# A two-layer transformer block on one core: another hand-written order for the drain of the attention and for the routed feed-forward behind it

## The chip, the core and the metric

The kernel runs on one core of a Trainium2 chip. TensorE (PE) multiplies matrices and transposes by multiplying with an identity; its results land in PSUM, a small memory which the kernel here cuts into buffers of 512 fp32 per partition. VectorE (DVE), ScalarE (ACT) and GpSimd (POOL) work on 128 partitions at a time; SyncE (SP) issues most of the transfers. Each engine runs its own list of instructions strictly in the order in which the kernel wrote them, and waits at an instruction until what it needs is there. The metric is device time in microseconds (us) from the first to the last instruction with what lies around it, here the median of several runs.

## The reference, cut to what matters

The input is `x`, 2 batches of 512 rows of 512 numbers. Two layers follow one another, each an attention and a feed-forward, each of these behind a layer norm that is scaled and shifted by numbers made from a conditioning vector (`mod`) and added to `x` through a gate. The change touches the last part of layer 1 only: the end of its attention, and its feed-forward.

```
h = layernorm(x) * (1 + cb) + sb
base_out = h @ base_W.T + base_b
probs = softmax(h @ router_W.T + router_b)        # 15 routes per row
topk_p, topk_i = top_k(probs, 8)
w = topk_p spread to the 8 experts by expert_map[topk_i]
lora = ((h @ A[e].T) * w[e]) @ B[e].T * 2          # rank 16 per expert, 8 experts
x = x + gb * (base_out + lora)
```

The attention of layer 1 has 128 heads with 4 numbers each, a latent of 64 and a rotary part of 64, and no mask; its scores are `exp(s - max)` and the sum is divided out at the end.

## The kernel before, in words

**Attention of layer 1.** The heads are taken four at a time in 64 units, called quads `t`; `Z` is the last one, `Z - 1` the one before it. A quad has four key blocks `i` and two pairs of heads `p`. For each `rope` multiplies the scores into PSUM (tile `s_i_p`, two halves of 512, pool `pS`, one buffer for each `p`), `keep` (ACT) copies them to SBUF, `largest` (DVE) takes the running maximum `mx`. When all blocks are in, `blocks`, `tops`, `twice` (DVE), `join` (a PE transpose), `top`, `top_hi`, `top_lo` (DVE) and `stripes` (POOL) bring the maxima into a layout from which `row` (PE) spreads each to a row `psm`; `row_copy` (ACT) makes SBUF copies of two of them. `less_...` subtracts the rows from the kept scores on DVE and POOL, `exponential` (ACT) follows, and `mix` (PE) multiplies with the values into `acc`. A planned order, `PLAN1`, lays the steps of neighbouring quads beside each other; `beside` hangs single steps of the feed-forward behind named steps of the plan near its end.

**The tail.** When the plan has run out, `tail()` lists by hand what is left, in the order in which every engine gets it: the end of quad `Z - 1`, the drain of quad `Z` (`part(i, odd)` does the subtractions and the exponentials of block `i`; with `odd`, DVE takes one more of the subtractions), `leave(Z)` and `last[...]`, which divide by the sums (`inverse`, `back`, `exact`, `spreading`, `scale`, `both`), then `projected(i)`, which multiplies with `Wo`, gates and adds to `x` for the four row tiles of batch 1.

**The feed-forward, class `Ffn1`.** Batch 0 has left the attention before, so its feed-forward can begin inside the drain; batch 1 has to wait for `projected`. For a batch `b`: `stats` (DVE) takes mean and variance of each row tile, `scale` (L370, L371) the root of the variance on ACT and its reciprocal on DVE, `rows(t)` (L385, DVE) the normalised rows `xn`; `turn(b, kc)` (L394 to L406) transposes them four tiles at a time on PE into a PSUM buffer and scales and shifts on the way out into `hT`, on ACT for even and on DVE for odd `kc`; `logits` (L412, 16 multiplications that the trace shows as 32 records) and `probs` (L433 to L437) make the exponentials of the routing; `chosen` (L444 to L464, DVE) normalises, compares each probability with each other (L451, 900 per partition) and counts ranks; `hidden` (L469) multiplies with the experts' first matrices; `weighed` (L485 to L490) turns the chosen weights and multiplies them in; `base(t)` (L499, 8 records) and `low(t)` (L509, 2 records) multiply into one PSUM tile per row tile, `leave(t)` (L520, L521) gates, adds and sends it out. `ready(f)` (L376) runs one tiny activation so that ACT loads the table of function `f` early.

**Buffers.** The pool `pX` has three PSUM buffers of 512 for everything small; `pS` has the two pairs of 512 that held the scores and later hold `base` and `low`. In the drain the rows `psm` 0 and 2 occupy two of the three `pX` buffers to the end, so the four transpositions of batch 0 share the third one.

**Where things stand before the change.** `scale(0)` hangs behind `exponential 0 0` of the plan, and `rows(0)`, `rows(1)` behind `tops 0`; `rows(2)`, `rows(3)` stand in the tail, ahead of `row`. The logits of batch 0 stand in one piece between `mix(Z, 1)` and `mix(Z, 2)`. `chosen(0)` stands in one piece between `scaled()` and `projected(0)`.

## Time and profile before

| what | value |
|---|---|
| runs | 2519.63, 2522.49, 2522.56 us; median 2522.49 us |
| the profiled execution | 2519.66 us, of which 2517.9 us are its span |
| mean granted TensorE clock | 0.985 |
| from 1000 to 2300 us | PE busy 1299.99 of 1300 us, clock 1.00 |
| from 2399 to 2439 us | PE busy 29.12 of 40 us, DVE 21.22, ACT 23.23, POOL 17.25, clock 0.68 |
| from 2439 to 2477 us | PE busy 31.06 of 38 us, DVE 25.43, ACT 6.39, POOL 11.15, clock 0.89 |
| from 2477 to 2518 us | PE busy 33.12 of 41 us, DVE 15.25, ACT 1.43, POOL 13.66, clock 0.85 |

The profile is one execution, recorded by the hardware. A page of it gives the busy time of each engine, and the chain that ended last, followed back from the last instruction: each piece of it is a start, a length and what ran then. A timeline lists the instructions of a stretch in order of time, with the wait ahead of each in brackets. A third view cuts a stretch into windows and gives for each the busy time of every engine and the granted TensorE clock as a share of full speed. Until 2399 us the core is bound by PE alone; the last 119 us are where the engines wait for each other, and the change lies in them.

### The profile page before, as it was taken

To read this page: it belongs to the slowest core of one execution; us is meant where nothing else is said; L and a number is where in the kernel's file an instruction comes from. 1 tells how busy PE (TensorE), PEld (TensorE's weight loads), DVE (VectorE), ACT (ScalarE), POOL (GpSimd) and SP (SyncE) were. 2 spreads that over 40 slices of the span, in tenths; PEclk is the share of its full clock that TensorE was granted. 3 is DMA by queue.
4 is the path that set the end of the run, shared out by engine and by line. 5 is a ranking of instruction groups with operands and counts; after the bars stand their busy time and mean duration, and the time that the engine had idled before them with its cause. 6 is when DMAs were issued, how large, how long until landed. Compare 5 with 4: busy or idle time off the path is not lost.

```text
span 2517.9 us, 28439 instructions
## 1 busy us (share of the span) xinstructions
PE 2453.7 (97%) x10252; PEld 1146.2 (46%) x10252; DVE 1684.2 (67%) x2309; ACT 1401.9 (56%) x2086; POOL 1571.9 (62%) x1521
## 2 busy tenths in 40 slices
PE   8999999999999899999999999999999999999877
PEld 3555555555555444444443444444344444444333
DVE  4445555555555435787778777778778877788764
ACT  2212112121221215888888788888888878888650
POOL 1333333333334323888888888888888888888643
PEclk9999999999999999999999999999999999999978
DMA  6211101001000100000000000000100000110000
GB/s 240 88 49 60 42 5 38 26 20 40 17 1 7 29 15 26 26 26 26 26 26 17 29 27 26 26 18 26 30 26 26 18 25 26 30 29 21 17 9 34
DMA packets 68697, 81.32 MB, mean 32 GB/s; under 512 B 6989, under 2 KB 49772, under 8 KB 68428
## 3 DMA queue, kind: packets, MB, share of 16 engines
q1 hardware_dynamic: 68348, 79.35, 10.1%
q8 instruction: 81, 1.33, 0.2%
q14 instruction: 60, 0.49, 0.1%
q0 software_dynamic: 208, 0.16, 0.0%
HBM read 77.40 MB, written 2.10 MB: 32 GB/s over the span
## 4 chain that ended last, share of the span: by engine, by line
PE 95%; DVE 3%; ACT 1%; DMA 0%; issue 0%; POOL 0%; SPq 0%; DVEq 0%; ACTq 0%; POOLq 0%
PE s L1081 19%; PE psq L1014 18%; PE acc L1236 10%; PE ps_q L685 9%; PE pw L797 8%; PE s L1090 5%; PE s L736 4%; PE po L783 4%; PE psv L707 2%; PE ps_k L685 2%; PE pt L772 2%; PE psu L1033 2%; PE psm L1160 2%; PE psw L1292 1%; PE psf L499 1%; PE psf L264 1%
## 5 line engine op out<-in xcount | busy, mean ns | idle before, releaser
L1187 POOL TENSOR_TENSOR ss<-ss,row 128x512 f32<-128x512 f32 x504 | 634.5, 1287 | 42.8 <-ACT row L1172 42.8
L1100 ACT COPY ss<-s 128x1024 f32<-128x1024 f32 x512 | 505.4, 1015 | 179.2 <-PE s L1090 130.5
L1081 PE MATMUL s<-q,ckr 64*128 64x512 f32 x2048 | 554.5, 612 | 10.7 <-ACT ss L1100 10.7
L1190 ACT ACTIVATE ss<-ss 128x1024 f32<-128x1024 f32 x512 | 525.2, 1070 | 5.6 <-DVE ss L1402 4.5
L1014 PE MATMUL psq<-hT,wqr 128*128 128x512 f32 x1024 | 466.7, 598 | 0.0
L1090 PE MATMUL s<-qm,c 64*128 64x512 f32 x1024 | 419.7, 795 | 0.4 <-DVE c L1051 0.4
L753 ACT ACTIVATE p<-s,nm 128x256 f32<-128x256 f32 (+1 forms) x256 | 110.9, 445 | 489.6 <-DVE nm L749 480.8
L1107 DVE TENSOR_TENSOR mx<-s,mx 128x1024 f32<-128x1024 f32 x256 | 306.6, 1218 | 41.2 <-PE s L1090 40.1
L695 POOL TENSOR_TENSOR qT<-t_q,t_q 128x512 f32<-128x512 f32 x64 | 81.2, 1269 | 402.6 <-DVE t_q L694 402.6
L1181 POOL TENSOR_TENSOR ss<-ss,rowe 128x512 f32<-128x512 f32 x252 | 317.9, 1285 | 0.0
L1014 PEld LDWEIGHTS psq<-hT,wqr 128*128 128x128 f32 x1024 | 189.0, 189 | 242.3 <-issue 211.7
L1081 PEld LDWEIGHTS s<-q,ckr 64*128 64x128 f32 x2048 | 184.1, 186 | 215.8 <-ACT ss L1100 97.3
L1236 PE MATMUL acc<-ss,vp 128*32 128x512 f32 x2048 | 266.9, 614 | 0.0
L1107 DVE TENSOR_TENSOR mx<-s,ss 128x1024 f32<-128x1024 f32 x128 | 156.7, 1224 | 117.1 <-ACT row L1172 79.7
L797 PE MATMUL pw<-wo,oT 128*128 128x512 f32 x512 | 230.3, 592 | 0.0
L685 PE MATMUL ps_q<-hT,wq 128*128 128x512 f32 x512 | 230.1, 592 | 0.0
L1112 DVE STREAM_TRANSPOSE mx<-mx 128x1024 f32<-128x1024 f32 x128 | 158.6, 1239 | 2.3
L1118 DVE TENSOR_REDUCE m<-mx 128x32 f32<-128x1024 f32 x128 | 156.1, 1219 | 4.4
L1090 PEld LDWEIGHTS s<-qm,c 64*128 64x128 f32 x1024 | 104.6, 187 | 118.8 <-issue 114.6
L1150 POOL TENSOR_TENSOR st<-mh,own_block 128x512 fp32r<-128x512 f32 x64 | 67.0, 1047 | 142.9 <-DVE mh L1146 142.9
L1183 DVE TENSOR_TENSOR ss<-ss,psm 128x512 f32<-128x512 f32 x252 | 155.7, 679 | 0.0
L685 PEld LDWEIGHTS ps_q<-hT,wq 128*128 128x128 f32 x512 | 96.0, 190 | 102.3 <-issue 100.6
(208 smaller groups left out, 3089.5 us busy)
## 6 DMA issues: line engine op xcount, KB each, us to landing
wqr<-in_L_attn_Wq_rope_pairs SPq DMA_DIRECT2D x64, 512.0 KB
wmod<-in_L_wmod SPq DMA_DIRECT2D x12, 1024.0 KB
wq<-in_L_attn_wq SPq DMA_DIRECT2D x8, 1024.0 KB
wo<-in_L_attn_wo SPq DMA_DIRECT2D x8, 1024.0 KB
x<-in_L_attn_x SPq DMA_DIRECT2D x8, 256.0 KB
wk<-in_L_attn_wk SPq DMA_DIRECT2D x8, 256.0 KB
wv<-in_L_attn_wv SPq DMA_DIRECT2D x8, 256.0 KB
out<-yf SPq DMA_DIRECT2D x8, 256.0 KB
```

The lines of the kernel that those rows point to most:

```text
L685: nc.tensor.matmul(ps, lhsT=wcols(kc), rhs=hT[b][:, kc, :], start=(kc == 0), stop=(kc == KC - 1))
L797: nc.tensor.matmul(ps, lhsT=oTs[u][:, hh, i * P : (i + 1) * P], rhs=groups[g]["o"][:, hh, :], start=(hh == 0), stop=(hh == GRP - 1),)
L1014: nc.tensor.matmul(ps, lhsT=wqs[t][:, kc, pair * P : (pair + 1) * P], rhs=hT[b][:, kc, :], start=(kc == 0), stop=(kc == KC - 1),)
L1081: nc.tensor.matmul(out[:, j, :], lhsT=whole[b]["kr"][r, bass.ts(i, P)], rhs=qs[t, p][r, :], start=True, stop=False,)
L1090: nc.tensor.matmul(out[:, j, :], lhsT=qkc[t // 2, 1][r, bass.ts(i, P)], rhs=qm[t, p][r, :], start=False, stop=True,)
L1100: nc.scalar.copy(ss[t, i, p], hold["s", t, i, p])
L1107: nc.vector.tensor_max(mx[t, p], hold["s", t, i, p], before)
L1112: nc.vector.transpose(m, m)
L1181: nc.gpsimd.tensor_sub(s, s, hold["r", t, 2])
L1187: nc.gpsimd.tensor_sub(s, s, hold["r", t, 2 * p + 1])
L1190: nc.scalar.activation(ss[t, i, p], ss[t, i, p], AF.Exp)
L1236: nc.tensor.matmul(accs[g, b][32 * h : 32 * (h + 1), :], lhsT=vps[t][:, kb, h, :], rhs=ss[t, kb, h // 2][:, h % 2, :], start=(s == 0 and k ...
```

## The change

Nothing is computed differently. Nine things are moved or regrouped:

1. `scale(0)` and all four `rows` of batch 0 leave the plan and its surroundings. `scale(0)`, with a `ready(Exp)` behind it that loads the table of the exponential again, now stands behind the last exponential of quad `Z - 1`; the rows stand between `row_copy` and `row(Z, 0)`.
2. `mix(Z - 1, 2)` and `mix(Z - 1, 3)` stand ahead of `row`, no longer behind it, and POOL's `less_odd(Z - 1, 1, 3)` ahead of `stripes(Z)`.
3. `turn` of batch 0 writes into the two pairs of `pS`, and has an argument for who reads it: ACT for the first of batch 0, DVE for the other three.
4. In `part(2, ...)` POOL takes back one subtraction from DVE.
5. The logits of batch 0 are made by row tile: two behind `mix(Z, 1)`, one behind `mix(Z, 2)`, one behind `leave(Z)`; `probs(0)` follows behind the first steps of the division.
6. `chosen` is cut into `compared` (the normalisation and the 900 comparisons), `ranked` (product and first sum) and `chosen` (second sum and the selection). For batch 0 these stand behind `base(0)`, behind `scale` and `both` of the division, and behind `rows` of batch 1.
7. The multiplication of the division's `spreading` stands between `base(0)` and `base(1)`, no longer behind both.
8. `hidden(0)` stands behind the four `projected`, no longer ahead of them.
9. For batch 1, `weighed(0)` stands between the third and the fourth `turn`, `low(0)` to `low(2)` behind `logits(1)`, `hidden(1)` ahead of `base(3)`, and `bias(1)` and the additions on POOL behind `weighed(1)`.

```diff
-        def turn(self, b, kc):
-            ps = self.pX.tile([P, S], F32, tag="x", name=f"pst1_3_{b}_{kc}")
+        def turn(self, b, kc, act):
+            if b:
+                ps = self.pX.tile([P, S], F32, tag="x", name=f"pst1_3_{b}_{kc}")
+            else:
+                if kc % 2 == 0:
+                    self.two = self.pS.tile(
+                        [P, 2, S], F32, tag=f"s{kc // 2}", name=f"pst1_3_{b}_{kc}"
+                    )
+                ps = self.two[:, kc % 2, :]
...
-            if kc % 2:
+            if not act:
...
-        def logits(self, b):
-            pl = self.pl[b] = self.pX.tile([P, TB, N1], F32, tag="x", name=f"pl{b}")
-            for i in range(TB):
+        def logits(self, b, tiles):
+            if 0 in tiles:
+                self.pl[b] = self.pX.tile([P, TB, N1], F32, tag="x", name=f"pl{b}")
+            pl = self.pl[b]
+            for i in tiles:
...
-            (Z + 1, "exponential 0 0"): [do(F.scale, 0)],
-            (Z + 1, "tops 0"): [do(F.rows, 0), do(F.rows, 1)],
...
+            less_odd(Z - 1, 1, 3)
             stripes(Z)
-            less_odd(Z - 1, 1, 3)
             F.low_weights()
             exponential(Z - 1, 1, 2)
             mix(Z - 1, 1)
-            F.rows(2)
-            F.rows(3)
+            exponential(Z - 1, 1, 3)
+            F.scale(0)
+            F.ready(AF.Exp)
+            mix(Z - 1, 2)
+            mix(Z - 1, 3)
             row(Z, 1)
             row(Z, 3)
             row_copy(Z, 0)
             row_copy(Z, 1)
+            for t in range(TB):
+                F.rows(t)
             row(Z, 0)
             row(Z, 2)
-            mix(Z - 1, 2)
-            exponential(Z - 1, 1, 3)
-            mix(Z - 1, 3)
             part(0, False)
-            for kc in range(2):
-                F.turn(0, kc)
+            F.turn(0, 0, True)
+            F.turn(0, 1, False)
             part(1, False)
             mix(Z, 0)
-            for kc in range(2, KC):
-                F.turn(0, kc)
-            part(2, True)
+            F.turn(0, 2, False)
+            F.turn(0, 3, False)
+            part(2, False)
             mix(Z, 1)
-            F.logits(0)
+            F.logits(0, (0, 1))
             part(3, True)
             mix(Z, 2)
-            F.probs(0)
+            F.logits(0, (2,))
             mix(Z, 3)
             leave(Z)
+            F.logits(0, (3,))
+            last[0](0)
+            F.probs(0)
             F.ready(AF.Sqrt)
-            last[0](0)
             last[1](0)
             last[2](0)
             F.base(0)
+            F.compared(0)
+            o = last[4](last[3]())
+            last[5](o)
+            F.ranked(0)
             F.base(1)
-            scaled()
-            F.chosen(0)
             F.bias(0)
-            F.hidden(0)
             projected(0)
...
             F.ready(AF.Exp)
+            F.hidden(0)
             F.base(2)
             for t in range(TB, NT):
                 F.rows(t)
+            F.chosen(0)
+            F.turn(1, 0, True)
+            F.turn(1, 1, False)
+            F.turn(1, 2, True)
             F.weighed(0)
+            F.turn(1, 3, False)
             for t in range(TB):
                 F.add_bias(t)
-            F.turn(1, 0)
-            F.turn(1, 1)
+            F.logits(1, range(TB))
+            F.probs(1)
             F.low(0)
             F.low(1)
-            F.turn(1, 2)
-            F.turn(1, 3)
-            F.logits(1)
-            F.probs(1)
+            F.low(2)
             F.leave(0, True)
             F.leave(1, True)
+            F.hidden(1)
             F.base(3)
-            F.low(2)
             F.low(3)
+            F.compared(1)
+            F.ranked(1)
             F.chosen(1)
-            F.hidden(1)
             F.leave(2, True)
             F.leave(3, True)
+            F.base(TB)
+            F.base(TB + 1)
+            F.weighed(1)
             F.bias(1)
             for t in range(TB, NT):
                 F.add_bias(t)
-            F.base(TB)
-            F.base(TB + 1)
-            F.weighed(1)
             for i in range(2):
```

More of the change, by code (lines that the diff above doesn't have):

```diff
@@ L437, in probs, with compared @@
             nc.scalar.activation(pr, pr, AF.Exp)
-        def chosen(self, b):
-            pr, (w, v) = self.pr[b], self.w
+        def compared(self, b):
+            pr = self.pr[b]
             rs = small.tile([P, TB], F32, tag="rs", name=f"rrs{b}")
@@ L446, in chosen, with ranked @@
             nc.vector.tensor_mul(pr, pr, rs.unsqueeze(2).to_broadcast([P, TB, N1]))
-            full = [P, TB, N1, N1]
-            w, v = (
-                x[:, : TB * N1 * N1].rearrange("p (t n m) -> p t n m", t=TB, n=N1) for x in (w, v)
-            )
+            self.full = [P, TB, N1, N1]
+            self.w = [
+                x[:, : TB * N1 * N1].rearrange("p (t n m) -> p t n m", t=TB, n=N1)
+                for x in self.w
+            ]
             nc.vector.tensor_tensor(
-                w,
-                pr.unsqueeze(2).to_broadcast(full),
-                pr.unsqueeze(3).to_broadcast(full),
+                self.w[0],
+                pr.unsqueeze(2).to_broadcast(self.full),
+                pr.unsqueeze(3).to_broadcast(self.full),
                 ALU.is_ge,
             )
-            before = self.before[:, :N1, :].unsqueeze(1).to_broadcast(full)
-            nc.vector.tensor_mul(v, w, before)
-            nc.vector.tensor_reduce(self.r1, v, AX.X, ALU.add)
-            nc.vector.tensor_reduce(self.r2, v.rearrange("p t n m -> p t m n"), AX.X, ALU.add)
+        def ranked(self, b):
+            before = self.before[:, :N1, :].unsqueeze(1).to_broadcast(self.full)
+            nc.vector.tensor_mul(self.w[1], self.w[0], before)
+            nc.vector.tensor_reduce(self.r1, self.w[1], AX.X, ALU.add)
+        def chosen(self, b):
+            over = self.before[:, N1, :].unsqueeze(1).to_broadcast([P, TB, N1])
+            nc.vector.tensor_reduce(
+                self.r2, self.w[1].rearrange("p t n m -> p t m n"), AX.X, ALU.add
+            )
             nc.vector.tensor_sub(self.r1, self.r1, self.r2)
-            over = self.before[:, N1, :].unsqueeze(1).to_broadcast([P, TB, N1])
             nc.vector.tensor_add(self.r1, self.r1, over)
-            nc.vector.scalar_tensor_tensor(self.psel, self.r1, E1 - 0.5, pr, ALU.is_lt, ALU.mult)
+            nc.vector.scalar_tensor_tensor(
+                self.psel, self.r1, E1 - 0.5, self.pr[b], ALU.is_lt, ALU.mult
+            )
         def hidden(self, b):
```

## The prediction

> **What bounds the kernel now.** The page comes first: PE is busy 97% of the span and holds 95% of the chain that ended last. That is true of the steady part and says little about this change. From 1000 to 2300 us PE is busy 1299.99 of 1300 us, and the two lists of instructions are the same up to 2399.8 us; so only the last 119 us can move, and they are read from the chain cut to that stretch (start, length, what):

> ```profile
> 2399.83 1.28 ACT L370
> ...
> 2405.31 1.39 DVE xn L385 x2
> ...
> 2412.24 1.05 POOL st L1150
> ...
> 2414.18 0.58 ACT row L1172
> ...
> 2419.16 1.05 PE pst L397 x4
> ...
> 2428.26 6.94 PE pl L412 x32
> 2435.20 3.57 PE acc L1236 x16
> 2438.78 7.96 PE psf L499 x16
> ...
> 2449.21 2.08 DVE rank L451
> ...
> 2453.54 1.58 DVE rank L460
> ...
> 2455.87 1.21 DVE y L1299 x2
> ...
> 2464.11 0.30 ACT rstd L370
> ...
> 2474.19 3.07 PE pl L412 x26
> 2477.26 5.23 PE psf L499 x8
> ...
> 2494.51 0.45 PE pselT_ps L485 x4
> ```

> The root of batch 0 (L370) and its rows (L385) sit in the chain of maxima; the logits (pl) hold up the last mixes (acc); the ranks of batch 0 (L451, L460) stand ahead of the projections (y) that batch 1 waits for. At the end it is PE again. The view of windows (length, busy PE, PEld, DVE, ACT, POOL, granted clock) adds that a busy PE isn't a fast one:

> ```profile
> 2430.00:2432.00 2.00, 2.00 (x11) 2.00 (x11) 1.09 (x2) 2.00 (x3) 0.00 (x0) 0.50 0.03 8
> 2442.00:2444.00 2.00, 2.00 (x7) 0.80 (x6) 0.15 (x1) 0.00 (x0) 0.61 (x1) 1.00 0.00 0
> ```

> At 0.50 the first logits took 6.94 us for 32 records (0.22 each), at 1.00 the second took 3.07 for 26 (0.12). An L499 record takes 0.43 at full clock and 0.86 at half; a mix of 8 records (half of the x16 above) 1.8 at half.

> **The sum, part by part.** I carry times of before forward through the new order, with the durations of the trace; "earlier" is against the trace.

> *1. The chain of maxima loses the root.* Gone from it are the wait of 2.15 us for L370, the reciprocal (0.18) and two rows (1.39). The maximum of block 3, pair 0, goes from 2401.55 to 2399.35 (DVE is free at 2399.31). Pair 1 goes from 2406.62 to 2403.1. Is its cover there? Its scores wait for ACT's copy, which without the root ends at 2400.8; PE needed 1.95 us from there, so 2402.8: just hidden. The stripes (POOL) go from 2412.24 to 2408.7, 3.5 earlier; `less_odd`, put ahead of them, runs 2406.8 to 2408.1 in time in which POOL waited 5.82 us.

> *2. ACT gets the root ahead of `row_copy`.* The last exponential of quad Z - 1 waits for that `less_odd` and ends at 2409.1. Then come two table loads, root and `ready`: 1.28 + 0.31 + 1.28 + 0.20 = 3.1 us. `row_copy` starts at 2412.2 instead of 2414.16; stripes and rows of PE were ready at about 2410.5, so this is the new last wait, and 1.5 of the 3.5 us are given back. [...]

> *3. DVE gets four rows together.* From 2411.0. One row costs 0.70 (2405.31) or 1.39 (at 2412.19, beside POOL's big subtractions), and 0.99 in batch 1. POOL is idle from 2409.8 until the row copies, so I take three at 0.7 and one near 1.2: done at 2414.2; ends 2413.8 and 2416.5. DVE's first two subtractions (0.68 each) end at 2415.7, before 2416.3. POOL's extra subtraction in part 2 (1.27, seven of them from 2412.8 to 2421.7) is beside others: DVE reaches part 2 later. That costs nothing unless POOL is over 3 us late.

> *4. Transpositions and mixes.* Before, two mixes of quad Z - 1 (3.57) stood between `row` and the first turn; now they are done by 2410. The transposition is at about 2414.9; ACT reads it behind two exponentials, at 2417.05 instead of 2420.24. The new PSUM pairs free less than they seem to: in the changed list of instructions each second turn of a pair still waits for the reader of the first. So: turn 1 at 2417.9, DVE 0.81, two subtractions, turn 2, DVE, turn 3, DVE: the last `hT` is written at 2423.5 (full clock) to 2424.9 (half); before it was 2427.5. From there before ran 32 logits and two mixes, 11.3 us. Now 16 + 8 records and two mixes at half clock: 3.5 + 1.8 + 1.75 + 1.8 with small waits, 9.7. The last mix ends at 2433.8 instead of 2438.78: **5.0 earlier.** The last 8 logits (1.75) follow it, so `base(0)` starts at 2435.6, only 3.2 earlier.

> *5. Ranks leave the way.* Before, y of the first projection started 17.1 us after the last mix, since DVE did 8 us of ranks first. Now PE decides: `base(0)` 5.1 (half its records at half clock), spreading 0.25, `base(1)` 3.45, first projection 0.86: y at 2445.3, before 2455.8. DVE's comparisons (2.07) end by 2441 and delay `scale` by half a us; `both` on POOL (1.27) ends at 2442.5, inside `base(1)`; `ranked` (2.2) inside it too. If `base(1)` were not there, these would cost 2 us. From y to the root of batch 1 before took 8.3; now 8.45, as the second projection is just in time. **Root at 2453.75, 10.4 earlier.** `hidden(0)`, now behind the projections, ends at 2449, and its copy on ACT waits behind root and load; nobody needs it before 2462.

> *6. What is given back.* Behind the root: rows as before (to +4.5 us), then the second rank sum and three small ones on DVE (1.66 + 0.75: +6.95), the transposed choice on PE (+7.6), ACT's copy behind its two `hT` (+8.2 to +8.75), the product (two records, 0.86 to 1.12: +9.1 to +9.9), only then turn 3, DVE's `hT` (+10.7 to +11.8), and the last 26 logits: 3.1 at full clock, 5.7 at half. So logits end at +13.9 to +17.5, before +13.15. The waiting turn 3 has all logits queued behind it. [...] Before, four wide records of `low` stood between the turns, and the clock was 1.00 from 2472 on; now there are none. By the rule +17.5, by the row of before +13.9; I take +16: **2469.75, 7.5 earlier.** Then the lows: behind the logits now stand three lows, not one, so 40 wide records instead of 36 until the second `weighed`: 4 x 0.43 = 1.7 back. The ranks of batch 1 start about 0.9 later behind the logits than they did (y waits for `low`), but end 8 us before PE asks for them. From 2494.51 on the order is the same (23.4 us to the end), POOL's additions included.

> Sum: 7.5 - 1.7 = **5.8 us earlier**. 2517.9 - 5.8 is a span of 2512.1, against its own execution 2513.9. That execution (2519.66) lies at the low end of the three runs; from the median, 2522.5 - 5.8 = **2516.7**.

> **Rivals.**

> *A. The clock stays full.* If the clock doesn't fall in the drain (turns and mixes packed) or between root and logits, step 4 gains up to 4 us more (24 logits and three mixes at 0.12 and 0.9 a mix) and step 6 up to 2. For: in before it was 1.00 from 2420 to 2426. Against: every stretch of logits in before ran into 0.50. Gain 9 to 12: 2511.5. Chance 0.18.

> [...] Chance 0.2.

> *C. Slower: the clock stays at half behind the drain.* Place: PE from the last logits to the fourth projection. There 8 + 8 records of base and 8 of projections stand before batch 1 can go on; all at half clock they cost 24 x 0.43 = 10.3 instead of the 1.7 that I count: 8.6 more, and the change would be 2.8 slower, 2525.3. It decides once 14 records more than I count are at half clock. For: a fully busy PE had 0.50 for 13 us from 2427 to 2440. Against: each time wide records came (2438.7, 2457.5, 2477), the clock rose within 4 us. Chance 0.1.

> *D.* That the order isn't what the source says can be left out: the built list shows the moves as described.

> **How the numbers follow.** The forecast has 0.52, with its own range from 2513 to 2519.5. The range for 8 in 10 reaches down into A and up over most of B: 2510 to 2522. A measurement of this kernel can't tell under 0.2%, 5 us, from no change. The forecast lies just beyond that; of its 0.52 I count 0.31 as faster and 0.21 as the same. With A (faster), B (same) and C (0.04 of it within 0.2%): faster 0.49, same 0.45, slower 0.06.

> **What would show it.** Step 1: stripes near 2408.7. [...] Step 3: rows of 0.7. Step 4: `acc` ends near 2434, the last logits behind it. Step 5: ten us from `base(0)` to the first y, DVE idle ahead of it; the root near 2454. Step 6: DVE's second rank sum ahead of `hT`, the last logits near 2470, the clock at 0.50 there. The prediction is wrong if the root of batch 1 isn't at least 7 us earlier, or if turn 3 waits more than 6 us behind the choice.

## The result, and the profile after

The changed kernel takes 2513.16 us (median of 6 runs, 2510.82 to 2516.18), the kernel before 2521.06 beside it (6 runs, 2517.6 to 2522.95): a ratio of 0.9971, 95% interval 0.9958 to 0.9983, or 7.9 us less. A later set of 18 runs gave a median of 2514.16 (2510.22 to 2519.24) and 0.9976 (0.9969 to 0.9983), 6.8 us less. The profiled execution took 2510.82 us, its span 2509.0.

The chain of waits of the changed kernel, cut to the same stretch (start, length, what):

```profile
2408.44 5.16 PE acc L1255 x24
2413.60 0.48 PE psm L1179
2414.08 0.58 ACT row L1191
...
2423.98 0.66 PE pst L404 x4
...
2425.63 1.89 PE pl L421 x16
2427.52 1.78 PE acc L1255 x8
...
2437.80 2.06 POOL o L1307
...
2441.93 0.70 DVE y L1318
...
2449.39 0.31 ACT rstd L370
...
2457.96 2.07 PE pw L508 x2
2460.03 1.04 PE pst L404 x4
2461.08 6.64 PE pl L421 x32
2467.72 4.55 PE psf L528 x6
...
2475.70 3.43 PE psf L518 x8
...
2486.86 0.45 PE pselT_ps L504 x4
```

The first root and its rows have left the chain, and of the comparisons and ranks ahead of y only the normalisation and the first half of the comparisons (0.52 us of L460) are left in it: y of the first row tile starts at 2441.07 (2455.79 before), and the root of batch 1 at 2449.39, against 2464.11. But ahead of the row copies stand 24 records of the mixes of quad Z - 1, 16 of which stood behind them before; and between the root and the second transposed choice (pselT_ps) lie 37.5 us where there were 30.4. So 14.7 us are won up to the root, and 7.1 are given back behind it.

The view of windows of the changed kernel (length, busy PE, PEld, DVE, ACT, POOL, granted clock) shows where PE is fast and where not:

```profile
2430.00:2432.00 2.00, 2.00 (x18) 1.14 (x18) 0.00 (x0) 0.65 (x2) 0.00 (x0) 1.00 0.00 0
...
2464.00:2468.00 4.00, 4.00 (x19) 4.00 (x19) 0.22 (x1) 0.00 (x0) 0.00 (x0) 0.50 0.02 4
```

The first stretch, at 0.50 before, is at full clock: from 2424 to 2454 it was 1.00. The logits of batch 1, at 1.00 before (3.07 for 26 records), now ran wholly at 0.50 (6.64 for 32).

**One execution is not the kernel.** The 18 further runs brought a second profiled execution of the same kernel, 2515.9 us with a span of 2514.1. Its chain has in the drain

```profile
2434.72 1.82 PE pl L421 x8
2436.54 4.91 PE psf L518 x8
...
2454.34 0.30 ACT rstd L370
...
2466.01 6.64 PE pl L421 x32
...
2492.01 0.45 PE pselT_ps L504 x4
```

with eight logits in 1.82 us, about twice the 0.99 of the other execution: its clock was 0.50 from 2419 to 2429 and from 2432.5 to 2439. The first profiled execution is the fastest of its six. To compare executions, times are counted here from an anchor that stands ahead of all edits, the second copy `g` of `psg` on ACT (2396.85 before, 2397.01 and 2398.52 in the two executions after). This matters: in the traces of this case the anchor lies between 2393.36 and 2400.93, so up to 7.6 us of the difference between two single executions arise where the kernels don't differ. "Half clock" is the sum of half-microsecond windows below 0.6 between 2395 and 2494.

| us behind the anchor | before | after | after, second | rows first | rows first, base(3) early |
|---|---|---|---|---|---|
| row copies start | 17.31 | 17.06 | 17.23 | 14.93 | 14.92 |
| ACT starts to copy the last mix of batch 1's attention | 42.07 | 34.43 | 36.35 | 31.39 | 31.58 |
| root of batch 1 | 67.26 | 52.38 | 55.82 | 49.35 | 49.54 |
| from that root to the second transposed choice | 30.40 | 37.47 | 37.67 | 36.50 | 30.98 |
| half clock | 36.0 | 31.5 | 39.5 | 23.0 | 19.5 |
| end of the span | 121.05 | 111.99 | 115.58 | 106.32 | 102.47 |
| the whole span | 2517.9 | 2509.0 | 2514.1 | 2505.0 | 2500.7 |

The last two columns are experiments that follow. The row copies of the changed kernel come hardly earlier than before; what its drain wins is won between them and the last mix (24.76 us before, 17.37 and 19.12 after). Part of that is the clock: before, the 32 logits there took 6.94 us, 0.22 each, and in the changed kernel the first 24 of them took 2.88 (0.12 each) and 3.24.

### The profile page after: what moved, and what is told of

The parts are those of the page before. It is cut to its first block, busy times and chain, and to the rows that moved or that the text cites. A ratio compares the mean times of both kernels' runs of the same rounds, so it can differ in the third digit from the quotient of the medians.

```text
span 2509.0 us, 28442 instructions
## 1 busy us (share of the span) xinstructions
PE 2447.4 (98%) x10252; PEld 1145.1 (46%) x10252; DVE 1681.4 (67%) x2309; ACT 1402.0 (56%) x2086; POOL 1576.9 (63%) x1522
## 4 chain that ended last, share of the span: by engine, by line
PE 95%; DVE 3%; ACT 1%; DMA 0%; POOL 0%; issue 0%; SPq 0%; DVEq 0%; ACTq 0%; POOLq 0%
PE s L1100 19%; PE psq L1033 18%; PE acc L1255 10%; PE ps_q L704 9%; PE pw L816 8%; PE s L1109 5%; PE s L755 4%; PE po L802 4%; PE psv L726 2%; PE ps_k L704 2%; PE pt L791 2%; PE psu L1052 2%; PE psm L1179 1%; PE psw L1311 1%; PE psf L264 1%; PE psr L101 1%
```

## The experiments

Ratios are to the kernel before, run beside each kernel on the same chip, with 95% intervals.

**Which half of the change carries the gain.** One kernel has the new drain (parts 1 to 5) and the old end, one the old drain and the new end.

```diff
# drain alone: behind base(0) the end of before
             F.base(0)
+            F.base(1)
+            scaled()
             F.compared(0)
-            o = last[4](last[3]())
-            last[5](o)
             F.ranked(0)
-            F.base(1)
+            F.chosen(0)
...
# end alone: the drain of before
+            (Z + 1, "exponential 0 0"): [do(F.scale, 0)],
+            (Z + 1, "tops 0"): [do(F.rows, 0), do(F.rows, 1)],
...
-            F.logits(0, (0, 1))
+            F.logits(0, range(TB))
```

> The new drain (root and rows, mixes ahead of row, turns, logits by tile), with the end of before behind it: ranks in one piece ahead of the projections, lows between the turns of batch 1. Theory 1 (the end's gain is given back by its own order: in the changed kernel y is 14.7 us earlier, 7.5 of them from the drain, but only 9.5 are left when the logits of batch 1 end and 7.6 at the second weighed): this kernel keeps most of the changed kernel's gain, 5 to 8 us faster than before, last mix near 2431 to 2434, root of batch 1 near 2456, second weighed near 2487. Rival (each half pays its part): 3 to 4 us faster than before.

> The drain of before (logits of batch 0 in one piece), with the new end: ranks in three pieces, spreading between the bases, lows and first matrices of batch 1 moved. Theory 1: the root of batch 1 comes 5 to 7 us earlier than before, but the late turn and the logits at half clock eat it: 0 to 2 us faster than before. Rival (each half pays its part): 4 us faster.

Drain alone: 2512.59 us (19 runs), 0.9967 (0.9958 to 0.9977). End alone: 2517.52 us (21 runs), 0.9988 (0.9981 to 0.9994). The two gains, 8.3 and 3.0 us by the ratios, don't add: together they bring 7.3 and 6 in the two sets of runs. On top of the drain the end adds nothing that these runs can tell. The stamps say why. Drain alone had the root of batch 1 59.56 behind the anchor and then needed 31.0 to the second transposed choice; end alone 60.04 and 36.2. From the copy of the last mix to the root it took 25.2 us before and in drain alone, 18.0 in end alone, and 17.95 and 19.47 in the changed kernel: taking the ranks off the way to the root, with the spreading between the two bases, is worth 5.7 to 7.2 us. The new order behind the root costs about as much, 5.8 to 7.3. These runs part the change into two halves only; the root's new place (part 1), POOL's subtractions (parts 2 and 4) and parts 6 to 9 were not undone one by one.

**What holds the row copies.** The chain put the 24 records of the mixes ahead of them. Here the last two mixes of quad Z - 1 stand behind the first transposition of batch 0.

```diff
             F.ready(AF.Exp)
-            mix(Z - 1, 2)
-            mix(Z - 1, 3)
             row(Z, 1)
...
             F.turn(0, 0, True)
+            mix(Z - 1, 2)
+            mix(Z - 1, 3)
             F.turn(0, 1, False)
```

> The changed kernel with the two last mixes of quad Z - 1 moved from ahead of row to behind the first turn. Theory 2 (in the changed kernel row_copy waits for PE, whose three mixes take 5.2 us at half clock ahead of row; ACT with its two table loads is done at 2412.1): row_copy starts at 2412.0 to 2412.5, 1.6 to 2 us earlier than in the changed kernel, the mixes fill PE's wait of 3.3 us before the second turn, and the last mix ends 1 to 2 us earlier; in all 1 to 2 us faster than the changed kernel, 9 to 10 us faster than before. Rival (the root on ACT holds row_copy, as the prediction said): row_copy stays where it is, the time does too.

2506.21 us (5 runs), 0.9943 (0.9931 to 0.9955). The timeline of the changed kernel (start, length, engine, line, operation, and in brackets the wait ahead of it), and below it that of this one:

```profile
2408.37 5.23 PE L1255 MATMUL acc<-ss,vp 128*32 128x512 f32 x24
...
2411.87 0.20 ACT L376 ACTIVATE tivationFunctionType.Exp<-eps_t 128x1 f32<-128x1 f32 x1
...
2413.53 0.73 PE L1179 MATMUL psm<-st,own_head 64*128 64x512 f32 x3
2414.07 1.08 ACT L1191 COPY row<-psm 128x512 f32<-128x512 f32 x2 [1.99 <-PE psm L1179]
...
2419.04 1.12 PE L404 MATMUL pst<-ident,xn 128*128 128x128 f32 x4 [3.25 <-ACT hT L413]
```

```profile
2412.30 1.22 PE L1179 MATMUL psm<-st,own_head 64*128 64x512 f32 x3 [0.35 <-POOL st L1169]
...
2413.50 0.20 ACT L376 ACTIVATE tivationFunctionType.Exp<-eps_t 128x1 f32<-128x1 f32 x1
2413.61 1.06 ACT L1191 COPY row<-psm 128x512 f32<-128x512 f32 x2
...
2416.00 3.13 PE L1255 MATMUL acc<-ss,vp 128*32 128x512 f32 x16
```

In the changed kernel ACT is through with its tables at 2412.07 and then waits 1.99 us for PE. With the mixes out of the way the copies follow ACT's last activation at once, 2.1 us earlier behind the anchor: PE's mixes were the wait. The reading is settled; its size was not. About 7 us are won on the changed kernel, not 1 to 2. The timeline shows one more thing: the mixes now fill the time in which PE waited 3.25 us ahead of the second transposition, and from 2418.5 on the clock is full for 34 us. In the profiled execution the row copies are the 2.1 us and the whole stretch behind the anchor is 5.7 and 9.3 us shorter than in the two of the changed kernel. How much of the rest is the clock and how much the shorter order isn't told apart here.

**What is given back behind the root.** Three kernels, each with one edit of the changed one.

```diff
# base(3) early
             F.base(2)
+            F.base(3)
...
-            F.base(3)
             F.low(3)
# weighed late
-            F.weighed(0)
             F.turn(1, 3, False)
...
             F.probs(1)
+            F.weighed(0)
# lows early
             F.weighed(0)
+            F.low(0)
+            F.low(1)
             F.turn(1, 3, False)
...
-            F.low(0)
-            F.low(1)
             F.low(2)
```

> The changed kernel with base(3) of batch 0 moved from behind hidden(1) to behind base(2), where PE waits over 3 us for the rows of batch 1. Theory 3 (what is left at the end is PE's own work behind the logits of batch 1): 3.4 us of it are taken out of the path at no cost, the clock stays full longer; 3 to 5 us faster than the changed kernel, 11 to 13 us faster than before, second weighed near 2483. Rival (the ranks of batch 1 on DVE, 12.4 us behind the logits, are next): not more than 1 to 2 us faster than the changed kernel, with PE waiting ahead of the second weighed.

> The changed kernel with weighed(0) moved from between the third and fourth turn of batch 1 to behind the logits and probs of batch 1. Theory 4 (what is given back behind the root is the turn that waits, 4.4 us from the end of turn 2 to the start of turn 3 in the changed kernel): turn 3 follows turn 2 by DVE's next hT, the logits end 3 to 4 us earlier, weighed then leaves PE waiting for 1.3 to 2.5 us ahead of the lows; 1 to 2.5 us faster than the changed kernel. Rival (only the half clock of the logits costs, 2.6 us, and it stays): the time stays within 1 us of the changed kernel's.

> The changed kernel with low(0) and low(1) moved from behind the logits of batch 1 to behind weighed(0), ahead of the fourth turn: four wide records more ahead of the logits. Theory 5 (the clock's half state at the logits is what the missing wide records cost): the logits take 4.1 to 5 us instead of 6.9, lows and first matrices behind them run at full clock, in all 1 to 3 us faster than the changed kernel although the turn waits 2 to 3 us longer. Rival (theory 4, the waiting turn): the turn waits longer, the logits end no earlier, 0 to 2 us slower than the changed kernel.

The kernel with `weighed` late changes part of the computation: `probs(1)` has bound the buffer of the choices anew by then, so batch 0 is multiplied with choices of batch 1 that are not yet made.

base(3) early: 2508.32 us (5 runs), 0.9947 (0.9934 to 0.9960). From the root to the second transposed choice its profiled execution needs 32.4 us instead of 37.5, so 5 us of the 7 given back are this one step: 3.43 are base(3) itself, and the logits end 16.5 us behind the root instead of 18.3. weighed late: 2513.61 us (8 runs), 0.9972 (0.9961 to 0.9982), the changed kernel's time; the fourth transposition no longer waits, but the logits again run at 0.50 (30 records in 6.59), the choice of batch 0 comes behind them instead, and root to choice stays at 37.9. Taking the wait away at that place gains nothing. Lows early: 2518.23 us (22 runs), 0.9984 (0.9976 to 0.9992). Its logits are faster (26 in 3.74), but four wide records (512 columns each) now stand ahead of the fourth transposition, and root to choice is 38.8: no gain. The median is 4 to 5 us above those of the changed kernel, but the interval of the ratio overlaps those of the changed kernel.

**Both edits together.** The mixes behind the first transposition, base(3) behind base(2); and the same with `weighed` late (it changes the same part of the computation).

> Both earlier moves together: the two mixes behind the first turn and base(3) behind base(2). They lie in different stretches (the drain, and behind the root of batch 1). If their gains add: 3 to 5 us faster than the mixes moved alone, 16 to 20 us faster than before, 2501 to 2505 us. If something else becomes last behind the logits (the ranks of batch 1 on DVE): less than 2 us faster than the mixes moved alone.

> The two moves and weighed(0) behind the logits. By theory 4, 1 to 2.5 us faster than the two moves without it, if the ranks of batch 1 (12.4 us behind the logits in the changed kernel, against some 14 us of PE's work there) do not become the last; by the rival the same or up to 1 us slower.

2503.52 us (5 runs, 2502.47 to 2505.29), **0.9934 (0.9922 to 0.9946)**: faster than both kernels, 17 us under the one before. With `weighed` late as well 2505.88 (5 runs), 0.9944 (0.9932 to 0.9956), nothing more. The chain of the faster one, behind its root:

```profile
2447.77 0.31 ACT rstd L370
...
2458.54 5.00 PE pl L421 x26
2463.54 4.06 PE psf L528 x6
2467.60 3.43 PE ph L488 x8
2471.03 0.86 PE psf L528 x2
2471.89 6.87 PE psf L518 x16
2478.75 0.45 PE pselT_ps L504 x4
```

The eight records of base(3), which stood in the changed kernel's chain at 2475.70 with 3.43 us, are gone from it: PE does them behind the root (the second half of the first line below), where it otherwise has only transpositions with waits of about 1 us between; these now run in one piece.

```profile
2445.25 7.03 PE L518 MATMUL psf<-wT,hT 128*128 128x512 f32 x16
...
2452.12 1.47 PE L404 MATMUL pst<-ident,xn 128*128 128x128 f32 x12
```

In the changed kernel PE has no wide record from 2450.5 to 2458.0, and its clock falls at 2454.3, 4.9 us behind the root; here the wide records reach to 2452.1 and the clock stays at 1.00 until 2459.4, 11.6 behind it. That is no accident of one execution: the four records of the first transposed choice took 0.60 us in three traces with base(3) early (alone, here, and with `weighed` late as well) and 0.83 to 1.03 in six that have the new end without it; in two of the six (rows first, end alone) the product behind it again took 1.14. One edit does two things at one place: it takes work from behind the logits, and it keeps the clock for the choice, its product (1.14 us instead of 2.07) and the fourth transposition. The logits themselves gain little: of the 26 that are left most still run at half clock (5.00 us; 5.73 with base(3) early alone).

**Two parts undone, and the changed kernel once more.** The transpositions of batch 0 in the one free buffer of pX (part 3), and the logits of batch 0 in one piece (part 5), in the changed kernel and in the fastest one.

```diff
# turns in pX
-            if b:
-                ps = self.pX.tile([P, S], F32, tag="x", name=f"pst1_3_{b}_{kc}")
-            else:
...
-                ps = self.two[:, kc % 2, :]
+            ps = self.pX.tile([P, S], F32, tag="x", name=f"pst1_3_{b}_{kc}")
# logits whole
-            F.logits(0, (0, 1))
+            F.logits(0, range(TB))
...
-            F.logits(0, (2,))
...
-            F.logits(0, (3,))
```

> The changed kernel with one part undone: the four transpositions of batch 0 share the one free buffer of pX again. Theory 1 (the pairs of pS bring nothing, since each second transposition of a pair waits for the reader of the first all the same): the times agree with the changed kernel's within 2 us, about 2513; the waits ahead of the second and of the fourth transposition stay near 3.2 and 0.9 us, the third waits in addition for DVE's copy of the second, but less than 0.5 us, because eight records of the mix run ahead of it. Theory 2 (the pairs let the third transposition and so ACT's and DVE's copies start earlier): the last hT is written 1 us or more later behind the anchor (the copy g of psg) and the time is 2 to 4 us above the changed kernel's.

> The changed kernel with one part undone: the logits of batch 0 in one piece of 32 records ahead of mix(Z, 2). Theory 1 (the 16 records that stood behind the last mixes are PE work that only moves, but the last mix and with it the division of batch 1 start later by their length): the last mix ends 1.9 to 2.2 us later behind the anchor where the clock is full (3.5 at half), base(0) starts at the same place, and since the division has base(0) and base(1), 7 us, to hide behind, at most 1 us reaches the end: about 2513 to 2514.5. Theory 2 (the division's DVE and POOL steps end just in time, psw waits for them): all of it reaches the end, 2515 to 2517.

> The fastest kernel so far (rows first, base(3) early) with the logits of batch 0 in one piece ahead of mix(Z, 2). There psw stands right behind base(1). Theory 1: the last mix ends 2 us later and psw waits for the division by less than that, the time is 2503 to 2505. Theory 2: psw waits by all of it, and the longer run of narrow records lets the clock fall to 0.50 in the drain again: 2506 to 2509.

> [...]

Turns in pX: 2512.11 us (11 runs), 0.9972 (0.9964 to 0.9981), beside 0.9976 of the changed kernel on the same chip. The waits ahead of the second and the fourth transposition are 3.19 and 0.91, with the pairs 3.25 and 0.91; the last mix is copied 36.36 behind the anchor, in the second execution of the changed kernel 36.35. The pairs of pS bring nothing that these runs show; each second transposition waits for the reader of the first in both.

Logits whole: 2510.74 us (5 runs), 0.9964 (0.9951 to 0.9977), not slower. The last mix is copied later, 37.61 behind the anchor, but `psw` starts at 46.08, in the second execution of the changed kernel at 46.43. The division of batch 1 has the 7 us of base(0) and base(1) to hide behind, and uses them up; that `psw` isn't later is also the clock, since base(0) ran at full clock here (3.70 us by the timeline, 5.07 in the second execution). In the fastest kernel the same edit gives 2504.95 (5 runs), 0.9936 (0.9924 to 0.9948) against 0.9934, and moves `psw` from 40.05 to 40.99 behind the anchor: at most 1 us. No run here shows that cutting the logits by tile makes the changed kernel faster, or that it costs time.

## Why the prediction was right, and where not

The forecast was 2516.7 us, a gain of 5.8; the runs show 7.9 and 6.8. (Of the distance to the measured 2513.16, 1.4 us are the kernel before, which was taken at 2522.5 and stood at 2521.06 beside the changed one.) Neither sign of being wrong came: the root was 14.7 us earlier, and the fourth transposition started 3.75 us behind the choice. By its steps:

*Step 1* was right in kind: the stripes came at 2409.55 where 2408.7 was forecast. The 0.85 are `twice` (L1145), which took 1.07 us where it had 0.20 before. What it ran beside is in the timeline of the changed kernel, and the same happens once more in step 5; behind it stand the two instructions that became longer as they were before:

```profile
2406.59 1.27 POOL L1206 TENSOR_TENSOR ss<-ss,row 128x512 f32<-128x512 f32 x1
2406.84 1.07 DVE L1145 COPY m<-m 128x64 f32<-128x64 f32 x1
...
2437.64 1.08 DVE L470 TENSOR_TENSOR rank<-rank,ffnc 128x900 f32<-128x900 f32 x1
2437.80 2.05 POOL L1307 TENSOR_TENSOR o<-o,r 128x512 f32<-128x512 f32 x1 [1.94 <-DVE r L1302]
```

```profile
2410.40 0.20 DVE L1126 COPY m<-m 128x64 f32<-128x64 f32 x1
...
2447.83 1.27 POOL L1288 TENSOR_TENSOR o<-o,r 128x512 f32<-128x512 f32 x1 [5.00 <-DVE r L1283]
```

DVE's copy ends 0.05 behind POOL's subtraction, and POOL's addition (1.27 before) ends 1.13 behind DVE's product, as if the later one had not begun until the earlier one was through. What lies behind this these runs don't show. The sum used the durations of before, and did not ask what runs beside them at the new places of `less_odd` and of the rank product.

*Step 2 is the one that failed.* ACT did what was forecast to a tenth: two loads of 1.28 each with the root directly behind the first, done at 2412.07 (2412.2 forecast); the first load begins where the exponential ends (2408.96), and the root 0.02 us behind the load's end (2410.26), so the price of before, 1.28 a load, stood. The upper end of the range reaches over rival B, a gain eaten in the drain; no run shows a cost of the loads beyond these 1.28, and 11.4 to 14.9 us were won up to the root. But "this is the new last wait" was wrong, and with it step 4's "now they are done by 2410". PE could not begin them before `psx` (2407.96), and the 24 records took 5.23 us, 0.22 each, at a clock of 0.50 from 2406.5 to 2413.4; so they ended at 2413.6 and `row` stood behind them in PE's order. The clock has its part in this: from a later mix of the same trace, 8 records in 1.07 us at full clock, 24 can be estimated at 3.2, and then `row` and ACT would have been ready at nearly the same time. The row copies came at 2414.07, not 2412.2. Moving the mixes behind the transposition took this wait away, with the clock at 0.50 there as well (2408.5 to 2418.5), and then the copies started directly behind ACT's table, as step 2 had it. The mixes ahead of `row` were read as a gain for the transposition, without asking what they themselves wait for and who is queued behind them.

*Step 3*: the four rows took 1.92 us (0.48 each), less than the 0.7 taken, with POOL idle throughout. DVE then waited 1.58 for `psm`, so the mistake of step 2 covered this gain.

*Step 4*: 36.95 behind the anchor was forecast for the last mix, at half clock. The execution in which the clock was at half has 36.35, the other 34.43. The end of the step held, though the row copies were 1.9 late (17.23 against 15.35): from them to the last mix it took 19.1 us where 21.6 had been worked out. That the two errors met is luck. What differs between the two executions is the first rival, "the clock stays full", in the drain only.

*Step 5*: the ranks left the way, as worked out. The root was forecast 56.90 behind the anchor, and came at 55.82 and 52.38. That PE decides before y held where the clock was at half; in the first execution POOL's `both` (2.05 instead of 1.27) ended last, 2439.86, and `psw` stood behind it.

*Step 6*, the give-back, was right in kind and too small. 16 us from root to the end of the logits were taken, between 13.9 and 17.5; both executions have 18.3. The clock was 0.50 through all 32 logits (6.64 us in both executions). No run here shows the rule by which the sum has +17.5; the traces show what went ahead in the first execution: from 2450.5 to 2458.0 PE had transpositions only, with waits of at most 1.08 us between them, and the clock fell at 2454.3. And the sum let only 26 logits count, with the first six hidden behind DVE's last `hT`; at half clock six take about 1.25 us, longer than the `hT` of 0.81, so all 32 counted. The lows then cost 1.9 against 1.7. The sum counted wide records behind the logits and did not ask whether PE had room for some of them in front: base(3) early takes 5 of the 7 us back.

So the gain forecast was made of a smaller gain up to the root (10.4) and a smaller give-back (4.6). Measured behind the anchor were 11.4 to 14.9 and 7.1 to 7.3, and 1.3 less at the end, where the order was the same and the clock was at half for one stretch of 3.41 us instead of 6.83. The two errors partly cancel, which is luck, and the range held the time for that reason too. The slower rival did not come: even where the drain ended at half clock, base(0) took 4.91 and base(1) 3.43 again. Its reading of before, that the clock rose within 4 us each time wide records came, was loose: behind the logits of 2474 the wide records began at 2477.26, the clock fell at 2478.1 and rose at 2481.5. So was the first rival's, that every stretch of logits in before ran into 0.50: the 26 records of 2474.19 to 2477.26 ran at 1.00.

## What to carry to other kernels

When a step is moved ahead of another on an engine that works in order, ask what the engine is waiting for at that moment and who stands behind the step: work put in front of a late-arriving, urgent instruction can delay it, while the same work put just behind it fills the wait that follows (the 16 records of the mixes: the row copies came 2.1 us earlier behind the anchor without them ahead of `row`, and PE's wait of 3.25 us was filled). When waits appear on PE in a tail, look for wide multiplications further back that need nothing new and put them there, unless something urgent then has to wait for them (as with the lows early); here they counted twice, as work gone from the path (the 3.43 us of base(3)) and for the clock (1.00 until 11.6 us behind the root instead of 4.9). Where two executions of one kernel differ by as much as the change is worth, compare stretches from a common anchor, and take the total from many runs.

## What was not expected of the hardware

A PE that was busy all the time did not bring the clock back in two stretches. From 2464 to 2468 PE was busy 4.00 of 4.00 us, nearly all of it with records of 15 columns, at 0.50; it returned to 1.00 only behind wide records (which began at 2467.72; the clock rose at 2471.4). Before the change 32 such records ran without a break at 0.50 from 2428.3 to 2435.2, and the clock rose at 2440.5, behind mixes and the first records of base(0).
